# Reordering the first and the fourth turn of a two-layer graph attention kernel

## The chip, the cores and the metric

The kernel runs on one core of a Trainium2 chip. The metric is the device time of one execution in microseconds (us), as the median over runs. The core has five engines that run on their own and wait for each other through semaphores: TensorE (PE in the profile, with its weight loads as PEld), VectorE (DVE), ScalarE (ACT), GpSimd (POOL) and SyncE (SP), which here issues every DMA.

## The reference, cut to what matters

Two layers run one after the other on x of shape (128, 128, 512) in float32, with a Boolean mask `adj` of shape (128, 128, 128). Each layer is attention over the 128 nodes of each of the 128 graphs, a residual sum and a normalisation.

```python
# layer 0: 4 heads of 64
q, k, v = split_heads(x @ Wq), split_heads(x @ Wk), split_heads(x @ Wv)
sim  = where(adj, (q @ k.T) * 64 ** -0.5, -finfo.max)
x    = layernorm(x + softmax(sim) @ v @ Wo + bo)
# layer 1: 8 heads of 64, with a layernorm of its own ahead
h    = layernorm(x) * gamma + beta
q, k, v = split(h @ w_qkv.T, 3)
s    = where(adj | eye, (q @ k.T) * 64 ** -0.5, -1e9)
x    = layernorm(x + softmax(s) @ v @ w_out.T + b_out)
```

## The kernel before, in words

Two graphs make a group, so there are 64 groups. The kernel is a software pipeline of turns, written out by hand: the recording order of the calls is the order of the instructions on each engine, and nothing is reordered later. `opening` (L878) holds the first three turns, `step(s)` (L961) each turn from the fourth (s = 3) to s = 63, and three closing functions the rest. In turn s a step makes layer 0's q, k and v of group s, the scores and softmax of group s-1, the attention output of group s-2, and layer 1's q, k, v of group s-3. The fourth turn is special: layer 1 starts in it, so layer 1's weights are still being prepared.

Each product of a matrix by a weight is cut into seven half-sized products, numbered 1 to 7, of sums of halves (a Winograd scheme). For layer 0 `product_0(g, i, ts=...)` (L505) issues the matmuls of product i; `ts` says which of q (0), k (1) and v (2). In the first three groups q, k and v have matmuls of their own; afterwards one matmul covers all three. The products are added up in three banks of PSUM: bank a takes 1, 6, 7 and 4 in turn, bank c takes 2, bank f takes 5 and 3. Between two products the bank is read ("tapped") by `taken_0` (L539): ScalarE copies it for products 1, 5, 6 (L553) and 4 (L555), and VectorE adds a kept copy for products 2, 3 and 7 (L558). A matmul that writes a bank waits for all reads of that bank that were recorded ahead of it. `hold=True` puts a read off until `flush(HELD)`, so that it is recorded later.

The sums of halves come from two helpers. `sums` (L364) has GpSimd make four of them from a group's transposed x (L376: the third and fourth instruction make the operands of products 3 and 7, the second that of product 6, the first that of 5). `weight_sums_0((t, i), ...)` (L249) has VectorE make the four sums of a weight t in order (L255 in `combine`, i = 0 to 3): i = 0 replaces an operand of product 5, i = 1 makes that of product 6, i = 2 of 7, and i = 3 of 4. `weight_sums` (L235, recorded as L247) does the same for layer 1, block 0 on GpSimd and block 1 on VectorE. ScalarE scales Wq by 1/8 in the opening (L890).

Other pieces that the change touches: `transposed(g)` (L107, recorded as L114) turns x of group g in VectorE's 32 x 32 blocks. `load_quarters(g)` (L95) issues the four DMAs that bring that x, into a buffer that the transposes of the group before must have left. `more_loads` (L218) issues the loads that come after. `turn_weights(n)` (L199, recorded as L194) turns n of 12 blocks of layer 1's weights on VectorE. `masked`, `maxima`, `exps`, `normalised` and `blocks` are the steps of the softmax of one part: VectorE copies the scores under the mask (L653) and takes the negated maxima (L659), ScalarE makes eight exponentials (L668), VectorE the reciprocal (L676), GpSimd the multiplication (L677), and VectorE the block transpose (L695), which goes through device memory and comes back for the attention product. `out_product(0, g, i, ...)` (L560, matmuls at L581) is the same seven-product scheme for the output weight; after each one VectorE adds the bank to the residual rows (L585), here called an output addition. `turn` (L287, transposes L292) and `arrive` (L296) send layer 1's normalised rows through device memory, and `finish` (L325) receives them on ScalarE. `stats` (L775) is the row statistics on VectorE, with roots on GpSimd (L789 to L804).

VectorE, ScalarE, GpSimd and SP work strictly in recorded order. In `step(3)` before the change, VectorE takes the maxima and the transposes of `turn(0)` ahead of the first output additions:

```python
maxima(s, 0, 1)
if s == 3:
    turn(s - 3)
    arrive(s - 3)
...
out_product(0, s - 2, 1, 2, 5)
```

Of the kernel before, what the change touches and what calls it, by code (L numbers as in the profile page):

```python
# [17 lines left out]
P = 128  # L18
# [9 lines left out]
def kernel(ctx: ExitStack, tc: tile.TileContext, x, adj, wq, wk, wv, wo, bo,  # L28
                            gamma, beta, w_qkv, w_out, b_out, out):
    nc = tc.nc  # L30
# [26 lines left out]
    def flush(what=later):  # L57
        while what:
            what.pop(0)()
# [19 lines left out]
    def load_rows(g):  # L79
        if 0 <= g < NG and g not in R:  # L80
            R[g] = five.tile([P, G, E], F32, tag="r", name=f"r_{g}")
            nc.sync.dma_start(R[g], x[g * G:(g + 1) * G].rearrange("b n e -> n b e"))
# [63 lines left out]
    wsqk = const.tile([P, 3, KH, I1], F32, name="wsqk")  # L146
# [52 lines left out]
    def turn_weights(n):  # L199
        for _ in range(n):  # L200
            blocks_in.pop(0)()
# [3 lines left out]
    load_mask(0)  # L205
    load_blocks(KQ.rearrange("p a w b c j -> p (a w b c j)"), 0, 4)
    wo0 = const.tile([P, INNER[0] // P, E], F32, name="wo0")
    nc.sync.dma_start(wo0, wo.rearrange("(c p) f -> p c f", p=P))
    bias0, bias1 = (const.tile([P, E], F32, name=f"bias{i}") for i in range(2))
    gb_raw = one.tile([2 * KC, P], F32, tag="sm2", name="gb_raw")  # L210
    gb = const.tile([P, 2 * KC], F32, name="gb")
# [5 lines left out]

    def more_loads():  # L218

        load_rows(0)  # L220
        nc.sync.dma_start(bias0, bo[None, :].to_broadcast([P, E]))
        load_mask(1)
        load_blocks(wsqk.rearrange("p i c f -> p (i c f)"), 4, 10)
        for i, of_feature in enumerate((gamma, beta)):
            nc.sync.dma_start(gb_raw[i * KC:(i + 1) * KC].rearrange("c (a i) -> c a i", i=32),
                              of_feature.rearrange("(a c i) -> c a i", a=4, i=32))
        load_rows(1)
        load_blocks(wsv.rearrange("p i c f -> p (i c f)"), 10, 12)
        load_transposed(wo1, w_out, "w_out", 0, 1, 2, 3)
        nc.sync.dma_start(bias1, b_out[None, :].to_broadcast([P, E]))  # L230
# [18 lines left out]
    def weight_sums_0(*which):  # L249

        for t, i in which:
            b11, b12, b21, b22 = (w0[:, c:c + KH, t, h] for c in (0, KH) for h in range(2))
            t2, t3, t4 = (ws0[:, j, :, t] for j in range(3))
            o, a, b = ((b12, b12, b11), (t2, b22, b12), (t3, t2, b11), (t4, b21, t2))[i]
            nc.vector.tensor_tensor(o, a, b, op=ALU.subtract)  # L255
# [108 lines left out]
    def sums(l, g):  # L364
        if not 0 <= g < NG:
            return
        xs = XS[l, g] = one.tile([P, 4, KH, N], F32, tag="xs1" if g == 1 else f"xs{l}", name=f"xs{l}_{g}")
        halves_sums(xs, XT[l, g].rearrange("p (h c) (b n) -> p b h c n", h=2, b=2))
# [134 lines left out]
    HELD = []  # L503
# [374 lines left out]
    def opening():  # L878

        sums(0, 0)  # L880

        k, qv = (1,), (0, 2)
        product_0(0, 1, ts=k)
        product_0(0, 2, ts=k, hold=True)
        weight_sums_0((1, 0), (1, 1))
        product_0(0, 5, ts=k)
        product_0(0, 3, ts=k, hold=True)
        product_0(0, 6, ts=k)
        for h in range(2):
            nc.scalar.activation(w0[:, :, 0, h, :], w0[:, :, 0, h, :], AF.Copy, scale=SCALE)  # L890
        weight_sums_0((1, 2), (1, 3))
        product_0(0, 7, ts=k)
        product_0(0, 1, 2, ts=(0,), take=())
        product_0(0, 4, ts=k)
        flush(HELD)
        weight_sums_0((0, 0), (2, 0))
        product_0(0, 1, 2, ts=(2,), take=qv)
        weight_sums_0((0, 1), (2, 1), (0, 2), (2, 2), (0, 3), (2, 3))
        product_0(0, 5, 6, ts=qv)
        transposed(1)  # L900
        product_0(0, 3, ts=qv)
        load_quarters(2)
        more_loads()
        sums(0, 1)
        cleared(1, 0)
        product_0(0, 7, ts=qv)
        product_0(1, 5)
        turn_weights(4)
        product_0(0, 4, ts=qv)

        product_0(1, 2, hold=True)
        product_0(1, 1)
        made = scores(1)
        cleared(2, 0)
        masked(made, 1, 0)
        maxima(1, 0)
        product_0(1, 6)
        product_0(1, 3, hold=True)
        transposed(2)
        sums(0, 2)  # L920
        load_ahead(3)
        flush(HELD)
        exps(1, 0, 0, 1)
        product_0(1, 7)
        product_0(2, 5)
        product_0(1, 4)
        normalised(1, 0)
        weight_sums_out(0)
        product_0(2, 2, hold=True)
        made = scores(2)  # L930
        load(2)
        blocks_direct(1, 0)
        masked(made, 2, 0)
        addend(0, 0)
        product_0(2, 1)
        maxima(2, 0)
        attend(2)
        out_sums(0, 0)
        product_0(2, 6)
        flush(HELD)  # L940
        cleared(3, 0)
        turn_weights(2)
        exps(2, 0, 0)
        out_product(0, 0, 1, 2, 5)
        product_0(2, 3)
        exps(2, 0, 1)
        out_product(0, 0, 6)
        normalised(2, 0)
        addend(0, 1)
        product_0(2, 7)  # L950
        out_product(0, 0, 3, 7)
        stats(0, 0, 0)
        product_0(2, 4)
        out_product(0, 0, 4)
        blocks_direct(2, 0)
        turn_gamma_beta()
        stats(0, 0, 1)
        transposed(3)
        turn_weights(2)

    def step(s):  # L961

        made = scores(s)
        if s > 3:
            sums(0, s)
            arrive(s - 3)
        if s > 3:
            flush()
        load_ahead(s + 1)
        load_rows(s - 1)  # L970
        masked(made, s, 0, 1, 2)
        attend(s)
        if s == 3:
            flush()
        maxima(s, 0, 1)
        if s == 3:
            turn(s - 3)
            arrive(s - 3)
        out_sums(0, s - 2)
        if s == 3:  # L980
            flush(latest)
            sums(0, s)
        if s > 3:
            exps(s, 0, 0)
        product_0(s, 1)
        exps(s, 0, *((0, 1) if s == 3 else (1,)))
        out_product(0, s - 2, 1, 2, 5)
        maxima(s, 2)
        product_0(s, 2)
        normalised(s, 0)  # L990
        out_product(0, s - 2, 6, 3)
        exps(s, 1, 0)
        stats(0, s - 2, 0)
        product_0(s, 6)
        exps(s, 1, 1)
        out_product(0, s - 2, 7)
        if s == 3:
            turn_weights(2)
        blocks(s, 0)
        if s == 3:  # L1000
            weight_sums(w1qk, wsqk, 0)
        product_0(s, 5)
        out_product(0, s - 2, 4)
        normalised(s, 1)
        finish(s - 3, 0)
        stats(0, s - 2, 1)
        exps(s, 2, 0)
        product_0(s, 7)
        finish(s - 3, 1)
        exps(s, 2, 1)  # L1010
        probs_arrive(s, 0)
        blocks(s, 1)
        product_0(s, 3)
        if s == 3:
            addend(0, s - 1)
            weight_sums(w1qk, wsqk, 1)
            turn_weights(2)
        product_0(s, 4)
        transposed(s + 1)
        turn_qk0(s)  # L1020
        if s == 3:
            prepare(len(setup))
        normalised(s, 2)
        qk(s - 3, 1)
        flush()
        qk(s - 3, 2)
        blocks(s, 2)
        arrive_qk0(s)
        probs_arrive(s, 1)
        qk(s - 3, 6)  # L1030
        if s == 3:
            weight_sums(w1v, wsv, 0)
        qk(s - 3, 5)
        flush(latest)
        addend(1, s - 5)
        out_sums(1, s - 5)
        qk(s - 3, 7)
        if s == 3:
            weight_sums(w1v, wsv, 1)
        qk(s - 3, 3, 4)  # L1040
        kq_arrive(s - 3)
        if s < NG - 1:
            probs_arrive(s, 2)
        out_product(1, s - 5, 1, 2)
        v(s - 3, 1, 2)
        turn(s - 2)
        if s == NG - 1:
            probs_arrive(s, 2)
        cleared(s + 1, 0, 1, 2)
        v(s - 3, 6)  # L1050
        out_product(1, s - 5, 6, 5)
        v(s - 3, 5)
        if s == 4:
            weight_sums_out(1, 0)
        out_product(1, s - 5, 7, 3, 4)
        q0_in_order(s)
        q_in_order(s - 3)
        if s > 3:
            addend(0, s - 1)
        v(s - 3, 7)  # L1060
        if s == 4:
            weight_sums_out(1, 1, 2)
        stats(1, s - 5, 0)
        v(s - 3, 3)
        if s == 4:
            weight_sums_out(1, 3)
        stats(1, s - 5, 1)
        v(s - 3, 4)
        for g in (0, 1) if s == 3 else (s - 2,):
            with_self(g)  # L1070
        if s == NG - 1:
            arrive(s - 2)
            addend(1, s - 4)
# [197 lines left out]
```

## Time and profile before

| what | value |
|---|---|
| runs | 2729.40, 2729.04, 2727.89 us |
| median of the runs | 2729.04 us |
| the profiled execution: its own time | 2727.97 us |
| its span in the trace | 2726.2 us |
| busy: PE, DVE, POOL, ACT | 2713.4, 2032.4, 1752.4, 1507.1 us |
| instructions | 47796 |

The profile is of one execution, 1.07 us below the median of the runs and within their spread of 1.5 us; 1.8 us of its time lies outside the span. A busy time is the sum of an engine's instructions. TensorE is busy for all but 12.8 us of the span, so a stretch of the trace says most by how long TensorE sat idle in it and by which engine let it go on. In the rows of the timeline the first number is the start, the second the length, both in us; "x4" means that four records are merged in one row, and a bracket at the end gives the idle time ahead and the engine that ended it.

### The profile page before, as it was taken

The numbers are of one execution on the slowest core, as the hardware profiler recorded it, in microseconds if no ns is written. First come the engines' busy times: TensorE is split into PE (matmuls) and PEld (weight loads), VectorE is DVE, ScalarE is ACT, GpSimd is POOL, SyncE is SP. The second block draws the span as 40 slices with busy tenths as digits, with TensorE's granted clock in tenths as the row PEclk, the third lists the DMA queues.
The fourth block names the chain that finished last, engine by engine and source line by source line (L and its number), as shares of the span: only waits on it lengthen the run. The fifth ranks groups of instructions, "written<-read, shape, count | busy, mean of one in ns | idle before, by whom it ended". The sixth has DMA issues, their size and how long they took to land.

```text
span 2726.2 us, 47796 instructions
## 1 busy us (share of the span) xinstructions
PE 2713.4 (100%) x14901; PEld 1927.3 (71%) x14901; DVE 2032.4 (75%) x3678; ACT 1507.1 (55%) x4804; POOL 1752.4 (64%) x2315
## 2 busy tenths in 40 slices
PE   8999999999999999999999999999999999999999
PEld 7866767667667676676776766767767667677698
DVE  7777777777777777777777777777777777777765
ACT  3456455465564554655646556556465565564654
POOL 5566666666666666667666666676666666666674
PEclk9999999999999999999999999999999999999999
DMA  8577777878777778787777777877777777777751
GB/s 188 149 215 212 220 214 203 225 209 217 214 209 217 215 209 224 207 219 210 209 219 216 209 221 208 220 211 209 217 214 211 223 206 218 214 208 219 208 151 67
DMA packets 588900, 562.64 MB, mean 206 GB/s; under 512 B 59368, under 2 KB 539112, under 8 KB 588648
## 3 DMA queue, kind: packets, MB, share of 16 engines
q1 hardware_dynamic: 588648, 559.59, 73.6%
q8 instruction: 120, 1.97, 0.3%
q14 instruction: 132, 1.08, 0.1%
HBM read 300.95 MB, written 258.47 MB: 205 GB/s over the span
## 4 chain that ended last, share of the span: by engine, by line
PE 98%; DVE 1%; issue 0%; POOL 0%; ACT 0%; DMA 0%; POOLq 0%; DVEq 0%; ACTq 0%; SPq 0%
PE qka L413 16%; PE a L531 12%; PE oa L581 12%; PE va L413 8%; PE qkf L413 8%; PE av L748 6%; PE of L581 6%; PE f L531 6%; PE vf L413 4%; PE qkc L413 4%; PE oc L581 3%; PE c L531 3%; PE sc L615 2%; PE sc L621 2%; PE vc L413 2%; PE sc_a L621 2%
## 5 line engine op out<-in xcount | busy, mean ns | idle before, releaser
L668 ACT ACTIVATE sm<-sm,nmax 128x128 f32<-128x128 f32 x1536 | 595.2, 393 | 4.1 <-DVE nmax L659 2.5
L677 POOL TENSOR_TENSOR sm<-sm,rec 128x1024 f32<-128x1024 f32 x192 | 364.3, 1897 | 334.7 <-DVE rec L676 331.3
L770 POOL TENSOR_TENSOR r<-r,bias 128x1024 f32<-128x1024 f32 x128 | 301.6, 2357 | 128.2 <-ACT r L769 128.2
L585 DVE TENSOR_TENSOR r<-oa,r 128x256 f32<-128x256 f32 x508 | 212.2, 418 | 159.7 <-PE oa L581 125.7
L668 ACT ACTIVATION_READ_ACCUMULATOR sm<-sm,nmax 128x1 f32 x1536 | 295.2, 192 | 0.0
L423 ACT COPY ev<-va 128x256 f32<-128x256 f32 x128 | 47.6, 372 | 432.8 <-PE va L413 432.7
L695 DVE STREAM_TRANSPOSE turnedp<-sm 128x1024 f32<-128x1024 f32 x188 | 233.4, 1241 | 62.3 <-POOL sm L677 59.2
L789 POOL TENSOR_SCALAR ve<-mv 128x2 f32<-128x2 f32 x191 | 41.8, 219 | 367.1 <-DVE mv L782 356.5
L815 ACT ACTIVATE r<-r,shift,root 128x512 f32<-128x512 f32 x254 | 193.0, 808 | 123.9 <-POOL shift L804 123.9
L659 DVE TENSOR_REDUCE nmax<-sm 128x8 f32<-128x1024 f32 x192 | 226.5, 1206 | 0.3
L413 PE MATMUL qkf<-w,xs 128*128 128x512 f32 x472 | 221.8, 592 | 0.0
L413 PE MATMUL qka<-wsqk,xs 128*128 128x512 f32 x472 | 221.8, 592 | 0.0
L581 PE MATMUL oa<-wso,so 128*128 128x256 f32 x760 | 205.8, 379 | 1.8 <-POOL xs L376 1.7
L581 PE MATMUL of<-wo,so 128*128 128x256 f32 x760 | 205.7, 379 | 0.3 <-DVE r L585 0.2
L376 POOL TENSOR_TENSOR xs<-xT 128x256 f32<-128x256 f32 x256 | 187.4, 732 | 22.7 <-DVE xT L114 21.2
L653 DVE COPY_PREDICATED sm<-m,sc 128x512 f32<-128x512 uint8 x256 | 172.4, 728 | 12.9 <-issue 4.2
L531 PE MATMUL f<-w,xs 128*128 128x384 f32 (+1 forms) x512 | 181.0, 476 | 0.0
L531 PE MATMUL a<-ws,xs 128*128 128x384 f32 (+1 forms) x512 | 181.0, 476 | 0.0
L581 PEld LDWEIGHTS oa<-wso,so 128*128 128x128 f32 x760 | 143.6, 190 | 48.0 <-POOL xs L376 2.3
L781 DVE BATCH_NORM_STATS2 st<-r 128x6 f32<-128x512 f32 x254 | 174.9, 688 | 2.2
L639 POOL MEMSET sm<- 128x1024 f32 x192 | 175.1, 952 | 1.4 <-DVE turnedp L695 1.4
L413 PEld LDWEIGHTS qka<-wsqk,xs 128*128 128x128 f32 x472 | 89.7, 190 | 112.9 <-issue 112.9
(176 smaller groups left out, 6312.5 us busy)
## 6 DMA issues: line engine op xcount, KB each, us to landing
scrp<-turnedp SPq DMA_DIRECT2D x188, 512.0 KB, 3.3
pT<-scrp SPq DMA_DIRECT2D x752, 128.0 KB, 3.5
kq<-scrkq SPq DMA_DIRECT2D x236, 192.0 KB, 3.9
x<-in_x_dram SPq DMA_DIRECT2D x256, 128.0 KB, 3.8
r<-in_x_dram SPq DMA_DIRECT2D x64, 512.0 KB, 4.2
out_dram<-r SPq DMA_DIRECT2D x63, 512.0 KB, 3.6
scr<-turned SPq DMA_DIRECT2D x62, 512.0 KB, 4.1
kq<-scr SPq DMA_DIRECT2D x248, 128.0 KB, 2.8
```

The source lines that it names most:

```text
L376: nc.gpsimd.tensor_tensor(o, a0, a1, op=op)
L413: nc.tensor.matmul(o, lhsT, rhs, start=first and m == 0, stop=m == len(todo) - 1, skip_group_check=True)
L531: nc.tensor.matmul(o, lhsT, rhs, start=first and n == 0, stop=n == len(todo) - 1, skip_group_check=True)
L581: nc.tensor.matmul(acc, left[:, c], right[:, c], start=first and c == 0, stop=c == hk - 1, skip_group_check=True)
L585: nc.vector.tensor_add(part, acc, part)
L639: nc.gpsimd.memset(sm, NEG1 if part else NEG0)
L659: nc.vector.tensor_reduce(NMAX[s, part], SM[s, part], AX.X, ALU.max, negate=True)
L668: nc.scalar.activation(sm[:, i, k, :], sm[:, i, k, :], AF.Exp, bias=nmax[:, i, k:k + 1], accum_out=total[:, i, k:k + 1])
L677: nc.gpsimd.tensor_tensor(SM[s, part], SM[s, part], rec[:, :, :, None].to_broadcast([P, 2, K1, N]), op=ALU.mult)
L695: nc.vector.transpose(t.rearrange("p q (h r) -> p q h r", r=32), SM.pop((s, part)).rearrange("p i k (q r) -> p q (i k) r", r=32))
L770: nc.gpsimd.tensor_tensor(R[g], R[g], (bias0, bias1)[l][:, None, :].to_broadcast([P, G, E]), op=ALU.add)
L815: nc.scalar.activation(R[g][:, b], R[g][:, b], AF.Identity, bias=shift[:, b:b + 1], scale=root[:, b:b + 1])
```

## The change

In the opening, for group 0, ScalarE's scaling of Wq moves ahead of its copy of product 6, product 6 moves ahead of product 3, and the q products 1 and 2 are issued ahead of k's product 7. The v products 1 and 2 are issued apart, around k's product 4, and the addition after product 2 is held. Group 1's transposes come ahead of four of the weight subtractions, and the held additions behind those. Group 2's transposes come a good deal earlier, and group 1's product 3 is not held any more. The load of Wo moves behind the loads of group 2's x. Two block transposes of layer 1's weights leave the end of the opening for the fourth turn.

In the fourth turn the maxima come behind the first three output additions, the exponentials behind product 2, `turn` and `arrive` behind the next two output additions, the normalisation behind two weight transposes, and GpSimd's first four weight sums behind the second statistics and two more weight transposes. From the fifth turn on nothing is changed.

```diff
     wo0 = const.tile([P, INNER[0] // P, E], F32, name="wo0")
-    nc.sync.dma_start(wo0, wo.rearrange("(c p) f -> p c f", p=P))
...
     def more_loads():
 
+        nc.sync.dma_start(wo0, wo.rearrange("(c p) f -> p c f", p=P))
         load_rows(0)
...
         product_0(0, 5, ts=k)
-        product_0(0, 3, ts=k, hold=True)
-        product_0(0, 6, ts=k)
         for h in range(2):
             nc.scalar.activation(w0[:, :, 0, h, :], w0[:, :, 0, h, :], AF.Copy, scale=SCALE)
+        product_0(0, 6, ts=k)
+        product_0(0, 3, ts=k, hold=True)
+        product_0(0, 1, 2, ts=(0,), take=())
         weight_sums_0((1, 2), (1, 3))
         product_0(0, 7, ts=k)
-        product_0(0, 1, 2, ts=(0,), take=())
+        weight_sums_0((0, 0), (2, 0))
+        product_0(0, 1, ts=(2,), take=qv)
+        product_0(0, 2, ts=(2,), take=qv, hold=True)
         product_0(0, 4, ts=k)
-        flush(HELD)
-        weight_sums_0((0, 0), (2, 0))
-        product_0(0, 1, 2, ts=(2,), take=qv)
-        weight_sums_0((0, 1), (2, 1), (0, 2), (2, 2), (0, 3), (2, 3))
+        weight_sums_0((0, 1), (2, 1))
         product_0(0, 5, 6, ts=qv)
         transposed(1)
-        product_0(0, 3, ts=qv)
         load_quarters(2)
         more_loads()
+        weight_sums_0((0, 2), (2, 2), (0, 3), (2, 3))
+        flush(HELD)
+        product_0(0, 3, ts=qv)
         sums(0, 1)
...
         product_0(0, 4, ts=qv)
+        transposed(2)
...
         product_0(1, 6)
-        product_0(1, 3, hold=True)
-        transposed(2)
+        flush(HELD)
+        product_0(1, 3)
         sums(0, 2)
         load_ahead(3)
-        flush(HELD)
...
         transposed(3)
-        turn_weights(2)
 
     def step(s):
...
         if s == 3:
             flush()
-        maxima(s, 0, 1)
-        if s == 3:
-            turn(s - 3)
-            arrive(s - 3)
+        if s > 3:
+            maxima(s, 0, 1)
         out_sums(0, s - 2)
...
         product_0(s, 1)
-        exps(s, 0, *((0, 1) if s == 3 else (1,)))
+        if s > 3:
+            exps(s, 0, 1)
         out_product(0, s - 2, 1, 2, 5)
-        maxima(s, 2)
+        maxima(s, 2 if s > 3 else 0)
         product_0(s, 2)
-        normalised(s, 0)
+        if s > 3:
+            normalised(s, 0)
+        else:
+            exps(s, 0, 0, 1)
         out_product(0, s - 2, 6, 3)
+        if s == 3:
+            turn(s - 3)
+            arrive(s - 3)
         exps(s, 1, 0)
...
         if s == 3:
             turn_weights(2)
+            normalised(s, 0)
         blocks(s, 0)
-        if s == 3:
-            weight_sums(w1qk, wsqk, 0)
         product_0(s, 5)
         out_product(0, s - 2, 4)
         normalised(s, 1)
         finish(s - 3, 0)
         stats(0, s - 2, 1)
+        if s == 3:
+            turn_weights(2)
+            weight_sums(w1qk, wsqk, 0)
         exps(s, 2, 0)
```

## The prediction

> **What bounds the kernel now.** I read the page's chain of waits first, then the busy times by stage, then the timeline of the stages in which TensorE (PE) idles.
>
> ```profile
> span 2726.2 us, 47796 instructions
> ...
> PE 98%; DVE 1%; issue 0%; POOL 0%; ACT 0%; DMA 0%; POOLq 0%; DVEq 0%; ACTq 0%; SPq 0%
> ```
>
> ```profile
> 8.00:20.30 12.30, 9.79 (x78) 8.76 (x76) 8.56 (x21) 3.22 (x9) 2.68 (x4) 1.00 1.18 226
> 20.30:36.80 16.50, 15.76 (x149) 15.12 (x149) 11.49 (x17) 5.95 (x22) 9.96 (x11) 1.00 1.03 209
> 36.80:50.00 13.20, 13.20 (x110) 12.18 (x108) 11.32 (x21) 6.22 (x22) 8.34 (x8) 1.00 1.03 228
> 50.00:69.30 19.30, 16.95 (x92) 11.51 (x92) 18.41 (x35) 9.80 (x29) 16.14 (x25) 1.00 0.39 118
> ```
>
> After each stretch and its length come the busy times of PE, PEld, DVE, ACT and POOL. PE idles 2.51, 0.74, 0.00 and 2.35 us here: 5.60 us, the most that the change can win. From 130 to 2600 us PE is busy 2470.00 of 2470.00 us, so every us by which PE is earlier or later at 69.3 us reaches the end unchanged. In the last stretch, DVE is busy 18.41 of 19.30 us: where PE idles there, DVE is the bound.
>
> ```profile
> 18.13 1.30 DVE L114 STREAM_TRANSPOSE xT<-x 128x512 f32<-128x512 f32 x2
> ...
> 19.50 0.72 POOL L376 TENSOR_TENSOR xs<-xT 128x256 f32<-128x256 f32 x1 [9.47 <-DVE xT L114]
> ...
> 20.28 1.16 PE L531 MATMUL f<-xs,w 128*128 128x128 f32 x8 [0.69 <-POOL xs L376]
> ...
> 31.51 1.13 PE L531 MATMUL f<-xs,w 128*128 128x128 f32 x8 [0.74 <-DVE qkv L558]
> ...
> 32.90 0.91 POOL L376 TENSOR_TENSOR xs<-xT 128x256 f32<-128x256 f32 x1
> 33.25 0.83 DVE L266 TENSOR_TENSOR wso<-wo 128x256 f32<-128x256 f32 x1
> ...
> 33.77 2.08 POOL L677 TENSOR_TENSOR sm<-sm,rec 128x1024 f32<-128x1024 f32 x1
> ...
> 34.12 2.00 DVE L266 TENSOR_TENSOR wso<-wso,wo 128x256 f32<-128x256 f32 x1
> ```
>
> Two PE waits of the opening stand here, and a rule of prices: a DVE subtraction from SBUF that takes 0.42 us alone ended 0.27 us after the POOL operation beside it (33.81 and 34.08; 35.85 and 36.12). Additions with a PSUM operand, and transposes, show no such delay.
>
> ```profile
> 55.26 1.22 DVE L659 TENSOR_REDUCE nmax<-sm 128x8 f32<-128x1024 f32 x1
> ...
> 56.39 1.29 DVE L292 STREAM_TRANSPOSE turned<-r 128x512 f32<-128x512 f32 x2
> ...
> 57.31 0.73 POOL L376 TENSOR_TENSOR xs<-xs,xT 128x256 f32<-128x256 f32 x1
> ...
> 57.61 0.38 DVE L585 TENSOR_TENSOR r<-oa,r 128x256 f32<-128x256 f32 x1
> ...
> 58.14 0.67 PE L581 MATMUL oa<-wso,so 128*128 128x256 f32 x2 [1.75 <-POOL xs L376]
> ...
> 60.01 1.90 POOL L677 TENSOR_TENSOR sm<-sm,rec 128x1024 f32<-128x1024 f32 x1 [0.48 <-DVE rec L676]
> ...
> 63.14 1.21 DVE L695 STREAM_TRANSPOSE turnedp<-sm 128x1024 f32<-128x1024 f32 x1
> ...
> 65.52 0.54 DVE L558 TENSOR_TENSOR qkv<-a,e 128x384 f32<-128x384 f32 x1
> ...
> 66.11 1.56 PE L531 MATMUL a<-ws,xT 128*128 128x384 f32 x4 [0.41 <-DVE qkv L558]
> ```
>
> The 1.75 us are put down to POOL, whose second sum ended at 58.04. Product 6 of the output does not read it; it writes the bank that DVE's first output addition reads until 57.99. DVE was late through the maxima and `turn`.
>
> **The opening, part by part.** All times are on before's clock. PE's pairs of matmuls follow each other at 0.45 us, 0.52 after a wait. Product 5 of k issues at 8.75 as now. Product 6 needs its weight sum (DVE, until 9.45): 9.58, then product 3 at 10.03, and the 0.45 us ahead of it goes. ScalarE scales Wq from about 9.85 (1.15 us; its load is in by 9.84, when a DMA that waits for it issues), and then copies product 6: 11.25. That is the new wait of q's product 1, with k's 7 queued behind: 11.40 against 12.58 before. Product 2 of q 11.92, k's 7 at 12.37, and DVE's addition until 13.38. Now v's product 1 waits for it: 13.48 (before 14.51), product 2 14.00, k's product 4 behind a copy of 0.37: 14.62, products 5 and 6 from 15.14 (before 15.51) until PE is free at 16.93 (17.54). So far 0.4 to 0.6 us are won, as four k waits fall into two.
>
> Then it is given back. DVE transposes group 1 at 15.0 to 16.4 (the x DMAs issued up to 9.84 land in 4.4 to 5.0 us). Behind them stand four subtractions, and behind those the held additions, for which product 3 now waits. But the transposes release POOL's four sums at 16.47, which before started at 19.50 when no subtraction was left. By the rows at 33 us one subtraction escapes (16.84), and each other ends 0.27 us behind a sum: about 17.6, 18.4 and 19.2. If they didn't meet, all four would take 1.5 us (17.46 and the row before it, 0.75 a pair): 17.9. The two additions end 0.45 us later, so product 3 issues at 19.7 to 19.8 (or 18.45) against 17.65, and group 1's product 5 four pairs later: 21.67 (or 20.3) against 20.28. Cost: +1.4 us, or 0 without the meeting. I take +1.4, as the pairing is that of the rows.
>
> The wait of 0.74 at 31.51 goes: group 2's transposes now run at about 24.8 instead of 29.16, its sums are done by 29.3, and product 3's addition follows at once, at 31.5. PE gets there at 21.67 + (30.61 - 20.28) = 32.00, so 0.90 of idle and restart are won: net +0.5. The output weight's subtractions (L266) meet POOL's long multiplication and addition one place earlier in their row, and end at about 39.2 against 38.63; the copy behind them gates the attention product. PE's wait there grows from about 0.1 to 0.35: +0.2. The moved load of Wo costs nothing: it issues near 18.5 instead of 13.71 and is read at 32.67, and this load landed in 7.5 us.
>
> **The fourth turn.** Two weight transposes leave its front, so DVE copies masks at 52.75 instead of 53.90. The output additions then come at 54.30, 54.79 and 55.17, as PE delivers them; the 1.75 us are gone. Maxima 55.5, product 2's addition 56.6, two output additions until 57.9. PE issues output products 6 and 3 at 56.2 and 56.7, and then waits for POOL's second sum, which is where it was: layer 0's product 6 at 58.15 against 59.51. So far 1.36 us are won.
>
> But DVE has the same work to do ahead of product 7's addition, plus two weight transposes that were done before: `turn` 57.95, statistics 59.17, output addition 60.2, transposes 60.5, reciprocal 61.72 (the exponentials end at 59.96). Only now can POOL normalise: 62.0 to 63.9. Before, DVE filled this time with statistics, an addition and weight transposes, and its block transpose at 63.14 found the result there since 61.91. Now the block transpose is next in the queue, and **DVE stands for 2 us**. Behind it: block transpose 63.97, output addition 65.1, statistics 65.5, weight transposes 66.35, and then product 7's addition, 67.57 to 68.11. PE has been ready for product 4 since 64.25 and issues it at 68.2, against 66.11: **+2.1 us**. All of the 1.36 is lost in that, since this wait ends last. Bounds: if the DVE steps ran without a gap from 52.75, 66.2 (+0.1); if POOL's multiplication took 2.08, +2.3.
>
> Behind that, POOL's weight sums (5.21 us) start behind the roots at 68.05 and now meet DVE's own four. They end at 73.3 to 73.7, and the second sum that the first layer-1 product 6 needs at about 75.1. PE is there 6.71 us after product 4, at 74.9: +0.2, bounds 0 and +0.8. `finish` is covered: `turn` ends 1.6 us later than before, and the first layer-1 product comes 2.1 us later.
>
> **Sum**: +0.5 + 0.2 + 2.1 + 0.2 = +3.0 on 2727.97: **2731.0 us**. The median of the runs is 1.07 above the profiled execution; against it the change is +0.07%, against its own execution +0.11%. Both are within 0.2% (5.5 us), about what a measurement of this kernel can tell from no change.
>
> **The rivals.** (1) The opening's subtractions escape the sums, because POOL starts later or x lands earlier: 1.4 us less, 2729.6. For it: DVE ran three such operations at 0.75 a pair when POOL was idle. (2) The gap of 3.7 to 4 us ahead of product 4 brings down the clock. In the tail the mean clock is 0.92 from 2720 to 2724 and 0.50 after, so it halved at about 2723.4, 2.9 us after the last matmul ended. If it takes 2.9 us of work to come back, half of that is lost: +1.4, 2732.4. Against it: the drop need not come at the same delay. [...] (3) Slower by over 0.2%: DVE's and POOL's layer-1 weight sums do not overlap at all, so that each POOL operation also waits for one of DVE's (0.69 each, L247). POOL then ends 4 x 0.69 = 2.8 us later, the sum for product 6 comes at 77.9, and PE waits 3 us: +5.8, 2733.8. It decides as soon as the sum is later than 74.9. Against it: in the opening POOL's 0.73 grew only to 0.78 and 0.90 beside subtractions. [...] (4) The change does what it says and DVE does not stand: product 4 at 66.2 or earlier, and without the opening's meeting 2727. A gain of 0.2% would need nearly all of the 5.60 us.
>
> **Chances.** Forecast 0.50, (1) 0.16, (2) 0.14, (3) 0.11, (4) 0.09, of which 0.01 is a gain over 0.2%. Slower by over 0.2% is (3) and a little of (2) with (3): 0.12; faster 0.01; within 0.87. The range leaves out (3)'s upper half and the lower half of (4): 2727.2 to 2734.5.
>
> **What would show it.** Right: in the changed trace PE's longest idle time in the fourth turn ends at layer 0's product 4 with DVE's L558 as releaser, after about 4 us; DVE idles 2 us ahead of L695 for POOL's L677; L255 subtractions of 0.8 us stand at 17 to 19 us beside L376; PE waits 2 to 3 us ahead of group 0's q and v product 3; none at group 2's product 5. Wrong: a block transpose that finds its data, subtractions of 0.42, or a clock below 1.00 between 60 and 75 us. It fails altogether if a stretch after 130 us shows PE idle.

## The result and the profile after

The changed kernel takes 2733.4 us in the median of 22 runs (2731.70 to 2734.69), the kernel before 2728.07 us (2727.68 to 2729.46, 22 runs). The ratio is 1.0017, with a 95% interval of 1.001 to 1.0024: 5.3 us slower by the medians, inside the 0.2% that were called no change, but with an interval that leaves 1 out.

The runs don't scatter evenly. Before has 15 runs at 2727.7 to 2728.4 and 7 at 2729.0 to 2729.5; the changed kernel has 9 at 2731.7 to 2732.2, 9 at 2733.4 to 2733.6 and 4 at 2734.2 to 2734.7. Its lowest group stands 3.9 us above before's lowest, and the rest of the 5.3 us lies in how many executions fall into the higher groups. The profiled execution is one of the lowest group: 2731.89 us, of which the span is 2730.1. What follows compares it with the profiled execution of before (2727.97 us, span 2726.2): 3.9 us in both.

The busy times by stage in the changed kernel; the columns are as in the prediction, and behind the busy times come PE's granted clock (1.00 in all of them), the share of the DMA engines and GB/s.

```profile
8.00:20.30 12.30, 8.54 (x65) 7.50 (x65) 9.16 (x18) 3.22 (x9) 5.81 (x8) 1.00 1.20 210
20.30:36.80 16.50, 16.50 (x160) 16.12 (x159) 11.55 (x18) 5.84 (x22) 6.90 (x8) 1.00 1.15 238
36.80:50.00 13.20, 13.20 (x109) 12.04 (x106) 11.63 (x21) 5.82 (x22) 8.01 (x8) 1.00 0.91 210
50.00:72.00 22.00, 17.52 (x98) 12.18 (x97) 18.91 (x34) 10.32 (x30) 14.30 (x25) 1.00 0.37 116
72.00:92.70 20.70, 19.35 (x152) 18.07 (x152) 16.06 (x28) 6.16 (x12) 15.60 (x18) 1.00 0.23 84
...
130.00:2600.00 2470.00, 2470.00 (x13030) 1711.99 (x13027) 1857.35 (x3349) 1384.98 (x4418) 1603.80 (x2116) 1.00 0.77 214
```

PE idles 3.76 us in the first stretch (2.51 before), none in the second (0.74), 4.48 in the fourth and 1.35 in the fifth. From 130 us on it is busy throughout, as before: nothing is given back later.

The longest waits of PE in the changed kernel: who waited for whom, the total in us, how often, the longest.

```profile
PE a L531 <- DVE qkv L558: 4.1, 2, 3.6
PE f L531 <- DVE qkv L558: 2.6, 1, 2.6
PE qka L413 <- POOL xs L376: 1.4, 1, 1.4
PE ready L139 <- POOL mhalf L133: 1.3, 1, 1.3
PE a L531 <- POOL xs L376: 0.8, 1, 0.8
PE a L531 <- ACT e L553: 0.5, 1, 0.5
```

Three waits matter: 3.6 at layer 0's product 4 of the fourth turn, 2.6 at group 0's product 3, and 1.4 at layer 1's first product 6. (The 0.8, at layer 0's product 6, is what is left of before's wait of 1.75 just ahead of it; the 1.3 is the same in both.) Here is the second of the three in the timeline.

```profile
14.91 1.30 DVE L114 STREAM_TRANSPOSE xT<-x 128x512 f32<-128x512 f32 x2 [0.31 <-DMA x<-in_x_dram]
...
16.14 1.25 DVE L255 TENSOR_TENSOR ws<-ws,w 128x256 f32<-128x256 f32 x2
...
16.30 0.82 POOL L376 TENSOR_TENSOR xs<-xT 128x256 f32<-128x256 f32 x1 [6.25 <-DVE xT L114]
...
17.32 1.80 DVE L255 TENSOR_TENSOR ws<-w,ws 128x256 f32<-128x256 f32 x2
...
19.25 0.27 DVE L558 TENSOR_TENSOR qkv<-f,e 128x128 f32<-128x128 f32 x1
...
19.57 0.71 PE L531 MATMUL f<-xs,w 128*128 128x128 f32 x4 [2.59 <-DVE qkv L558]
...
21.46 1.08 PE L531 MATMUL f<-xs,w 128*128 128x128 f32 x8
...
31.70 1.06 PE L531 MATMUL f<-xs,w 128*128 128x128 f32 x8
```

A pair of subtractions takes 1.25 and 1.80 us beside the sums, and ends 0.27 and 0.29 us after a sum (16.30 + 0.82, 18.05 + 0.78). Before, GpSimd was idle beside them and a pair took 0.75:

```profile
17.46 0.75 DVE L255 TENSOR_TENSOR ws<-w,ws 128x256 f32<-128x256 f32 x2
```

Group 1's product 5 is at 21.46, 1.18 later than before; group 2's, without its wait, at 31.70, only 0.19 later. The fourth turn of the changed kernel:

```profile
62.09 0.16 DVE L676 RECIPROCAL rec<-total 128x8 f32<-128x8 f32 x1
62.33 1.90 POOL L677 TENSOR_TENSOR sm<-sm,rec 128x1024 f32<-128x1024 f32 x1 [2.39 <-DVE rec L676]
...
64.26 1.25 DVE L695 STREAM_TRANSPOSE turnedp<-sm 128x1024 f32<-128x1024 f32 x1 [2.01 <-POOL sm L677]
...
67.87 0.52 DVE L558 TENSOR_TENSOR qkv<-a,e 128x384 f32<-128x384 f32 x1
...
68.44 1.56 PE L531 MATMUL a<-ws,xT 128*128 128x384 f32 x4 [3.65 <-DVE qkv L558]
```

VectorE stands for 2.01 us in front of the block transpose, and everything behind it in its queue is late by that. Then the weight sums of the two engines, and PE's next wait:

```profile
69.72 1.61 POOL L247 TENSOR_TENSOR wsqk<-w 128x512 f32<-128x512 f32 x1
...
70.22 1.65 DVE L247 TENSOR_TENSOR wsqk<-w 128x512 f32<-128x512 f32 x1
...
71.40 1.59 POOL L247 TENSOR_TENSOR wsqk<-wsqk,w 128x512 f32<-128x512 f32 x1
...
71.91 1.64 DVE L247 TENSOR_TENSOR wsqk<-wsqk,w 128x512 f32<-128x512 f32 x1
...
75.89 0.73 POOL L376 TENSOR_TENSOR xs<-xs,xT 128x256 f32<-128x256 f32 x1
...
76.67 1.05 PE L413 MATMUL qka<-xs,wsqk 128*128 128x128 f32 x7 [1.35 <-POOL xs L376]
```

Before, the two rows of sums stood apart, and one such sum took GpSimd 1.27 us and VectorE 0.69:

```profile
63.22 1.27 POOL L247 TENSOR_TENSOR wsqk<-w 128x512 f32<-128x512 f32 x1
...
67.66 0.69 DVE L247 TENSOR_TENSOR wsqk<-w 128x512 f32<-128x512 f32 x1
...
72.82 1.95 PE L413 MATMUL qka<-xs,wsqk 128*128 128x128 f32 x16
```

Layer 1's first product 6 was at 72.82 and is at 76.67. That is 3.85 us, so practically the whole difference of 3.9 is there by then.

### The profile page after: what moved, and what is told of

Read it like the earlier page. It is cut to its first block, busy times and chain, and to the rows that moved or that the text cites. A ratio compares the mean times of both kernels' runs of the same rounds, so it can differ in the third digit from the quotient of the medians.

```text
span 2730.1 us, 47795 instructions
## 1 busy us (share of the span) xinstructions
PE 2713.1 (99%) x14901; PEld 1927.0 (71%) x14901; DVE 2035.6 (75%) x3678; ACT 1507.5 (55%) x4804; POOL 1753.0 (64%) x2315
## 4 chain that ended last, share of the span: by engine, by line
PE 98%; POOL 1%; DVE 0%; DMA 0%; issue 0%; SPq 0%; POOLq 0%; DVEq 0%
PE qka L413 16%; PE a L531 12%; PE oa L581 12%; PE va L413 8%; PE qkf L413 8%; PE av L748 6%; PE of L581 6%; PE f L531 6%; PE vf L413 4%; PE qkc L413 4%; PE oc L581 3%; PE c L531 3%; PE sc L615 3%; PE sc L621 2%; PE vc L413 2%; PE sc_a L621 2%
## 5 line engine op out<-in xcount | busy, mean ns | idle before, releaser
L815 ACT ACTIVATE r<-r,shift,root 128x512 f32<-128x512 f32 x254 | 193.0, 808 | 122.9 <-POOL shift L804 122.9
```

The source lines that it names most:

```text
L815: nc.scalar.activation(R[g][:, b], R[g][:, b], AF.Identity, bias=shift[:, b:b + 1], scale=root[:, b:b + 1])
```

## The experiments

The theory: three places make the loss, each by the order of the work and not by added work. In the opening the held additions stand behind subtractions that GpSimd's sums hold up; in the fourth turn VectorE stands in front of the block transpose; and then the weight sums of VectorE and GpSimd hold each other up. On top of these, PE's clock drops in some executions, in the gaps that were made. Rivals: one of the two turns carries the whole loss; VectorE simply has too much work in the fourth turn; the runs' groups have nothing to do with PE. Each median is set beside that of the kernel before on the same chip.

### Each turn alone

The opening alone is the changed kernel's opening with `turn_weights(2)` at its end, and before's `step`; the fourth turn alone is before's opening without that call, and the changed `step`.

> Only the opening is changed; the two weight transposes stay at its end, and the fourth turn is that of before. Theory: the opening wins 0.6 us by its earlier product waits and 0.9 at group 2's product 5, and gives back 1.2 to 1.4 at group 0's product 3, so that PE is 0.2 to 0.4 us later at 50 us: 2728.3 to 2728.6 where before is 2728.1. Rival (the opening carries the whole loss of the change, the fourth turn none): 2733.4.

> Only the fourth turn is changed, with the two weight transposes that it takes over; the opening is that of before. Theory: product 4 of layer 0 is 1.9 to 2.1 us later and layer 1's first product 6 another 1.4 to 1.5: +3.4 to +3.6, 2731.6 in undisturbed executions and 1.6 to 2.7 more where the clock drops in the gap of 3.6 us ahead of product 4. Rival (the opening carries the loss): 2728.1.

Measured: the opening alone 2730.04 us (2728.68 to 2731.64, 11 runs), before 2728.35 (27 runs), ratio 1.0006, interval 0.9997 to 1.0015. The fourth turn alone 2731.59 us (2731.26 to 2732.67, 11 runs), ratio 1.0013, interval 1.0004 to 1.0021. So both rivals fall: neither turn carries the whole. The fourth turn hit its number: 7 of its runs lie at 2731.3 to 2731.7. Its upper group, 2732.4 to 2732.7, is only 1.0 higher, where 1.6 to 2.7 were expected. The opening hit its number only in its best run, 2728.68; its median is 1.4 to 1.7 us over the expected span. In its trace PE gets to group 2's product 5 at 31.82, so 0.31 later than before, as the theory has it. The rest shows further on, behind the wait of the old fourth turn:

```profile
58.65 0.67 PE L581 MATMUL oa<-wso,so 128*128 128x256 f32 x2 [1.73 <-POOL xs L376]
59.51 0.83 PE L581 MATMUL of<-wo,so 128*128 128x256 f32 x2 [0.19 <-DVE r L585]
...
68.16 1.56 PE L531 MATMUL a<-ws,xT 128*128 128x384 f32 x4 [0.26 <-DVE qkv L558]
```

Product 4 is at 68.16 where 66.6 would follow. The same kernel by stretches (the third number from the right is the granted clock):

```profile
58.00:60.00 2.00, 1.16 (x4) 0.79 (x5) 1.72 (x5) 2.00 (x11) 1.92 (x3) 0.97 0.47 195
60.00:62.00 2.00, 2.00 (x4) 1.04 (x4) 1.61 (x4) 0.21 (x2) 1.54 (x2) 0.50 0.18 70
62.00:64.00 2.00, 2.00 (x6) 1.33 (x5) 0.55 (x3) 0.48 (x1) 1.92 (x3) 0.67 0.83 252
```

The clock is halved from about 59.9 to 63.3 us, behind a gap of 1.7. The 1.5 us by which product 4 is late is about what a halved clock over these 3.4 us costs (an estimate: half of it, 1.7). That is the prediction's clock rival, at a place that it had not named, and the runs on the clock below test it.

### The block transpose later

```diff
         if s == 3:
             turn_weights(2)
             normalised(s, 0)
-        blocks(s, 0)
+        else:
+            blocks(s, 0)
...
         product_0(s, 7)
+        if s == 3:
+            blocks(s, 0)
         finish(s - 3, 1)
```

> The changed kernel, with the block transpose of the fourth turn recorded behind product 7, so that VectorE no longer stands in front of product 7's addition until GpSimd has normalised. Theory (VectorE's standing makes the gap ahead of product 4): the addition is 3 us earlier, PE's wait there falls from 3.65 to 0.5 to 1 us, but GpSimd's roots and weight sums are moved up by less, so that 1.5 to 2 us wait remain at layer 1's first product 6: 2.4 us less than the changed kernel, 2729.4 to 2730. Rival (the gap is made by the amount of work, two more weight transposes of 1.3 us ahead of the addition): the wait stays over 2.4 us and the time within 1 us of 2731.9.

Measured: 2729.49 us (2729.25 to 2731.33, 11 runs), before 2728.35, ratio 1.0005, interval 0.9996 to 1.0014. PE's waits in its trace:

```profile
65.38 1.56 PE L531 MATMUL a<-ws,xT 128*128 128x384 f32 x4 [0.51 <-DVE qkv L558]
74.22 2.05 PE L413 MATMUL qka<-xs,wsqk 128*128 128x128 f32 x16 [1.96 <-POOL xs L376]
```

The wait at product 4 falls from 3.65 to 0.51 with the same instructions on VectorE ahead of it, save the block transpose: of the 3.14 us, 2.01 were the standing and most of the rest the transpose's own 1.25. So VectorE was not simply full: the two weight transposes are still ahead of the addition. Product 4 is 3.06 us earlier, but layer 1's product 6 only 2.45, as its wait grows from 1.35 to 1.96. That second wait is what the next run is about.

### The weight sums apart

```diff
-                    eng=nc.gpsimd if w is w1qk and c == 0 else nc.vector)
+                    eng=nc.vector)
...
             turn_weights(2)
-            weight_sums(w1qk, wsqk, 0)
...
-            weight_sums(w1qk, wsqk, 1)
+            weight_sums(w1qk, wsqk, 0, 1)
```

> The changed kernel, with all eight of layer 1's weight sums for q and k on VectorE, in one row where VectorE had its four, so that GpSimd has none and can't meet them. Theory (the wait of 1.35 us at layer 1's first product 6 comes from the two engines' sums holding each other up): GpSimd's second sum is ready by 71 us, the wait goes, VectorE's eight take 5 to 6 us against 6.4 for the four now, and the time is 1.3 us less than the changed kernel. Rival (the wait comes from the late arrival of layer 1's rows): the wait of 1.35 stays and the time with it. Third: VectorE's longer row makes a later product wait, and the time is the same or up to 1 us more though the first wait is gone.

Measured: 2738.25 us (2737.87 to 2740.03, 5 runs), before 2728.35, ratio 1.0039, interval 1.0025 to 1.0053. This is a miss in the time: the expected 1.3 us less than the changed kernel's lowest group became 6.4 more. Its first half came as the theory had it: GpSimd's second sum ended at 70.5, and PE had no wait at layer 1's product 6. But VectorE's row took 9.5 us, not 5 to 6, as it met GpSimd's sums of x and then the addition of the bias, which held one subtraction for 2.84 us:

```profile
72.74 2.80 POOL L770 TENSOR_TENSOR r<-r,bias 128x1024 f32<-128x1024 f32 x1
...
73.25 2.84 DVE L247 TENSOR_TENSOR w<-w 128x512 f32<-128x512 f32 x1
...
85.31 0.68 DVE L500 SCALAR_TENSOR_TENSOR qo<-qka,eqk 128x512 f32<-128x512 f32 x1
...
86.04 3.58 PE L413 MATMUL qka<-xT,wsqk 128*128 128x128 f32 x16 [1.99 <-DVE qo L500]
```

Everything behind it on VectorE was late, and layer 1's product 4 waited 1.99 us for an addition, the third case of the expectation in a larger size. And the clock fell twice: the four matmuls of layer 0's product 4 took 2.10 us instead of 1.56 (the clock is 0.81, 0.50 and 0.84 in the stretches from 68 to 74 us), and the product after the wait took 3.58 instead of 1.95 (the clock is 0.57 in both stretches from 86 to 90 us). These losses don't make up the whole 6.4 either: set beside the changed kernel's, the trace is 3.86 us late at 131 us, 4.9 at about 1307 and 6.3 at the end. What adds 2.4 us over the later turns stays open.

The run shows that the wait of 1.35 came from GpSimd's row of weight sums, and that this is no way to mend it. As GpSimd has no row left here, it can't tell by itself whether the row was late by the meeting or by its own length. The rows of the changed kernel do: without growth it would have ended at 68.37 + 5.21 = 73.58, and the second sum of x, 1.53 later by before's rows, at about 75.2, when PE was there (75.3). A kernel further below shows the two cases side by side.

### The clock

Matmuls of the identity, into a bank that nothing reads, fill the gaps and leave nothing out; the second kernel has both lines, the first only that of the fourth turn.

```diff
+    def fill(n, name):
+        warm = mm_tile(name)
+        for _ in range(n):
+            nc.tensor.matmul(warm[:, :P], ident, ident, start=True, stop=True, skip_group_check=True)
...
         flush(HELD)
+        fill(9, "warm_open")
         product_0(0, 3, ts=qv)
...
             weight_sums(w1qk, wsqk, 1)
             turn_weights(2)
+            fill(14, "warm_turn")
         product_0(s, 4)
```

> The changed kernel, with 14 matmuls of the identity into an unread bank recorded ahead of product 4 in the fourth turn, about 3.2 us of work that fills most of the gap of 3.65 us there. It adds work and leaves nothing out. Theory (the executions at 2733.4 and 2734.6 are those in which PE's clock drops in a gap): if this gap is the cause, runs gather at 2731.7 to 2732.2 and those at a mean clock of 0.998 are gone or few. Rival (the spread of 3 us has another cause, as a DMA or the launch): the three groups stay as they are. Third: the gap in the opening causes part, and the group at 2733.4 stays while the one at 2734.6 goes.

> As the run before, with 9 more such matmuls, about 2 us, ahead of group 0's q and v product 3 in the opening, where PE idles 2.6 us. Theory: all runs within 0.5 us of 2731.9, as no gap over 1.5 us is left before the tail. Rival (neither gap has to do with the spread): three groups up to 2734.6.

Measured: with the fourth turn's gap filled 2733.49 us (11 runs), with both filled 2731.89 (11 runs), before 2728.30. By single runs: with one gap filled, 3 runs at 2731.7 to 2731.9 and 8 at 2733.0 to 2733.7, none higher; with both, all 11 at 2731.65 to 2732.16. The third case of the first expectation is what came: the highest group goes with the fourth turn's gap, the middle one with the opening's. The first half of that is the weaker one: 4 runs of 22 became 0 of 11, which chance alone would give in about one case of nine. That no run of 11 is left in either upper group with both gaps filled, where 13 of 22 were, can hardly be chance: the spread comes from the two gaps, and traces show PE's clock drop at them. The profiled execution of the first kernel is one of the middle group (2733.49 us) and shows the drop:

```profile
18.00:20.00 2.00, 0.49 (x4) 0.49 (x5) 1.79 (x5) 0.00 (x0) 2.00 (x3) 1.00 1.22 210
20.00:22.00 2.00, 2.00 (x16) 2.00 (x15) 0.42 (x1) 0.00 (x0) 1.42 (x2) 0.73 1.18 197
22.00:24.00 2.00, 2.00 (x12) 2.00 (x11) 1.90 (x4) 0.00 (x0) 0.00 (x0) 0.50 1.04 348
24.00:26.00 2.00, 2.00 (x18) 2.00 (x18) 1.40 (x3) 0.85 (x2) 0.00 (x0) 0.92 1.09 338
```

From the means the clock is halved from about 20.9 to 24.3 us, 3.4 us long, and begins 1.4 us after PE has gone back to work at 19.5, behind a gap of 2.45 us in this run. By an estimate it costs half of 3.4 us, 1.7, and the groups are 1.6 apart.

The last run on this takes the kernel before and fills its wait of 1.75 us, with `fill(7, "warm_turn")` ahead of `out_product(0, s - 2, 6, 3)` in the fourth turn.

> The kernel before, with 7 matmuls of the identity into an unread bank, about 1.6 us, recorded ahead of the output products 6 and 3 of the fourth turn, where PE waits 1.75 us; nothing is left out. Theory (the kernel before also has executions in which the clock drops in a gap, and this is the gap): the runs at 2729.0 to 2729.7 go, and all lie at 2727.6 to 2728.5. Rival (they come from somewhere else, as the opening or the tail): both groups stay.

Measured: 2727.98 us, all 11 runs at 2727.72 to 2728.25, while the unchanged kernel on the same chip had 6 of 20 at 2729.2 to 2730.2. So before's upper group came from that gap; that the clock was the reason is argued from the other traces, as none of before's was taken in that group.

### The opening and the fourth turn mended

In the opening, on the changed kernel:

```diff
-        weight_sums_0((0, 2), (2, 2), (0, 3), (2, 3))
         flush(HELD)
+        weight_sums_0((0, 2), (2, 2))
         product_0(0, 3, ts=qv)
...
         product_0(1, 5)
+        weight_sums_0((0, 3), (2, 3))
         turn_weights(4)
```

> The changed kernel with the held additions ahead of the weight subtractions again, and the four subtractions split in two pairs, each ahead of the product that needs it. Theory (product 3 waits for additions that stand behind subtractions that GpSimd's sums hold up): product 3 issues at about 17.0 instead of 19.57, group 1's product 5 at 18.9 instead of 21.46, and everything after is 2.3 to 2.6 us earlier: 2729.4 in undisturbed executions. Rival (the additions are late because the transposes are, not because of the subtractions): product 3 stays over 18.5 and the gain is under 1 us.

Measured: 2730.69 us (2729.28 to 2731.20, 11 runs), before 2728.30, ratio 1.0007, interval 0.9998 to 1.0016. Product 3 issues at 16.99 and group 1's product 5 at 19.64, so 1.82 us earlier and not 2.3 to 2.6: product 7 still waits a little for subtractions beside GpSimd's sums (a pair takes 1.85). The best run lies at the expected 2729.4, the median above it, and the profiled execution (2731.19) shows why: the gap ahead of product 4 is still there, and this time the clock falls inside it, at about 65.4, and stays halved until 72.2, so for 6.8 us (means of 0.84, three times 0.50, and 0.95 in the stretches from 64 to 74 us).

```profile
61.51 1.45 PE L531 MATMUL f<-w,xs 128*128 128x384 f32 x4
66.61 2.93 PE L531 MATMUL a<-ws,xT 128*128 128x384 f32 x4 [3.65 <-DVE qkv L558]
69.34 3.30 PE L156 MATMUL w_outt<-ident,raw_v 128*128 128x128 f32 x16
72.48 1.95 PE L413 MATMUL qka<-xT,w 128*128 128x128 f32 x16
```

The two rows take 5.87 us from start to start where the changed kernel's took 3.14 (68.44 to 71.58). Of the 2.7 us lost, about half costs nothing, as layer 1's product 6, which would have waited 1.35, waits no more.

Then the fourth turn, on top of that kernel:

```diff
         if s == 3:
-            flush(latest)
             sums(0, s)
+            flush(latest)
...
-            turn_weights(2)
             normalised(s, 0)
-        blocks(s, 0)
+            turn_weights(4)
+            weight_sums(w1qk, wsqk, 0)
+        else:
+            blocks(s, 0)
...
-        stats(0, s - 2, 1)
-        if s == 3:
-            turn_weights(2)
-            weight_sums(w1qk, wsqk, 0)
+        if s > 3:
+            stats(0, s - 2, 1)
...
         finish(s - 3, 1)
+        if s == 3:
+            blocks(s, 0)
+            stats(0, s - 2, 1)
```

> The kernel of the run before, and in the fourth turn: normalisation ahead of the weight transposes, all four of these in one row, GpSimd's weight sums right behind its multiplication, block transpose and second statistics behind product 7, the sums of x ahead of the ratios. Theory: the waits at product 6 (0.84), product 4 (3.65) and layer 1's product 6 (1.35) go, and one of up to 0.8 us comes at layer 1's first product, which waits for the rows that go through device memory: 2724 us, 4 us less than before. Rival (VectorE is simply full in the fourth turn, so that a wait taken away comes back at the next product): no better than before, 2728.

Measured: 2726.06 us (2725.48 to 2727.19, 11 runs), before 2728.30, ratio 0.9992, interval 0.9984 to 1.0001. The three waits are gone; 2.2 of the 4 us came. Three of GpSimd's weight sums now run ahead of VectorE's and keep their length (1.27, 1.27 and 1.28 us). The fourth still meets them, and grows as in the changed kernel:

```profile
63.20 1.28 POOL L247 TENSOR_TENSOR wsqk<-wsqk,w 128x512 f32<-128x512 f32 x1
...
64.44 1.72 POOL L247 TENSOR_TENSOR wsqk<-w,wsqk 128x512 f32<-128x512 f32 x1
...
65.07 1.65 DVE L247 TENSOR_TENSOR wsqk<-w 128x512 f32<-128x512 f32 x1
```

So the meeting makes the growth. Of the 1.8 us that didn't come, 1.1 went into a wait that was not foreseen: the later statistics made GpSimd's roots late, ScalarE's normalisations (L815) wait for them, and ScalarE's copy of layer 1's product 6 stands behind these.

```profile
PE qka L413 <- ACT eqk L425: 1.1, 1, 1.1
```

The last kernel records the `flush()` of the normalisations behind layer 1's product 7 instead of behind product 1 (s = 3 alone).

> The kernel mended in both turns, with the layer 0 normalisations of the fourth turn on ScalarE recorded behind layer 1's product 7 instead of behind product 1. Theory (in the mended kernel PE waits 1.12 us for ScalarE's copy of layer 1's product 6, which stands behind normalisations that wait for late roots): the wait goes and the time is 1.0 to 1.1 us less, 2725.0. Rival (the copy is late for another reason, or the next product waits in its place): 2726.0.

Measured: 2724.84 us, all 11 runs at 2724.48 to 2725.20, before 2728.22 (20 runs), ratio 0.9986, interval 0.9977 to 0.9995. Its longest waits of PE are 1.3 us at the very start and 0.5; from 50.0 to 69.3 us PE is busy 19.08 of 19.30. It beats both kernels: 3.4 us under before, about 8.6 under the changed one.

## Why the prediction was right, and where it was off

**The chain to the forecast held.** The opening wins early, loses at group 0's product 3 and wins at group 2's product 5: it is 0.19 us late at 31.70 and 0.40 late at 50 us, where +0.7 was forecast (+0.5 and +0.2). Both ends were forecast 0.2 to 0.3 us too late: product 5 of group 1 at 21.46 for 21.67, of group 2 at 31.70 for 32.00. The meeting of subtractions and sums is there in the rows; taking the two apart gave 1.8 us. The signs that were named for being right are all in the trace.

**The fourth turn's standing** came as forecast: layer 0's product 6 at 58.50 (58.15 and the 0.40), VectorE idle 2.01 us (forecast 2), product 7's addition at 67.87 (67.57 plus the 0.40 by which PE came late is 67.97), product 4 at 68.44, PE's wait 3.65. That is 1.93 us on top of the opening's, forecast +2.1. The run with the block transpose later shows the cause.

**The mis-sized term is the layer-1 weight sums**: forecast +0.2 with bounds of 0 and +0.8, measured +1.52 (3.85 less 2.33), so outside its own bounds. The place and the mechanism were right. The price was taken from the opening, where GpSimd's operation of 0.73 grew to 0.78 and 0.90; here its 1.27 grew to 1.59 to 1.72, so that its row ended at 74.68 instead of 73.3 to 73.7, and the first sum of x behind it took 1.17 beside VectorE's last subtraction. VectorE's operations here are longer (0.69 alone against 0.42), and a POOL operation that met one grew by about half of it. The rival with full exclusion (+2.8 on the row) was too dear in turn: the row grew from 5.21 to 6.31. One VectorE and one GpSimd operation in turn, without overlap, would be 0.69 + 1.27 = 1.96 us a pair, by an estimate from their lengths in the kernel before. The sums start 1.56 to 1.69 us after each other in both rows, so about half of the way to full exclusion; which part of an operation overlaps with the other's is not shown.

**The sum** for an execution with an undisturbed clock was +3.0 on the profiled execution's own time, and +3.9 came. The median of the runs moved by 5.3, because the clock rival (0.14) is not a rival but an addition, by the filled gaps in 13 of 22 executions. The step that failed there is in its condition: one gap was named, that of product 4, with a drop 2.9 us behind the last matmul. The opening's gap of 2.6 us was worked out in the same text and not counted, and before's 1.75 us, too, go with an upper group of about a third of the executions. In two traces the clock was halved for 3.4 us (59.9 to 63.3 with the opening alone, 20.9 to 24.3 with the fourth turn's gap filled), behind gaps of 1.73 and 2.45 us. Half of 3.4 us, 1.7, is an estimate of the loss, and agrees with the 1.6 between the groups.

The range held the time with little to spare, 2733.4 under 2734.5, and that is partly luck: its upper end had been left for a part of rival (3), and what used it up was a loss 0.9 larger than forecast with the clock undisturbed, and about 1.5 more by the clock. The 0.87 for no change held just as narrowly, 5.3 us against a bound of 5.5. The runs tell the two kernels apart better than that: the interval of the ratio begins at 1.001. The +0.07% was reckoned against a median of three runs, two of which lay in before's upper group; of 22 runs the median is 2728.07, close to the profiled execution.

**Left open**: which of the middle group's executions had a drop in the opening and which a long one in the fourth turn. The opening's gap gave 1.6 us; the fourth turn's, where it stood alone, 1.0 by the groups of its runs, or nothing. Only profiled executions show which it was. Open, too, are the 2.4 us that the kernel with all sums on VectorE lost over its later turns.

## What to carry to other kernels

In a queue that works in strict order, the price of an instruction that must wait is paid by everything recorded behind it (here VectorE stood for 2.01 us, and PE's wait behind it grew from 0.41 to 3.65 us): ask what stands there and who needs that, before asking how long the wait is. When an edit brings two engines' rows side by side that were apart before, price them by a pair that was caught side by side with operations of the same length. Here a gap on TensorE of 1.7 to 3.7 us cost its own length and, in a share of the executions, 1.0 to 1.6 us more, so count all gaps, and look at single runs and not the median alone.

## What was not expected of the hardware

The clock dropped behind gaps shorter than the 3.4 us for which it then stayed halved: 1.73 us of waiting (then halved from 59.9 to 63.3 us) and 2.45 us, where the drop began 1.4 us after PE had resumed. With that wait of the fourth turn filled by about 1.6 us of matmuls of the identity, the kernel before lost its upper group (none of 11 runs, where 6 of 20 were in it).

One drop was free: in the fourth turn the slow matmuls used up time that the next product would have waited anyway, so the kernel with the fourth turn alone shows a halved clock from about 69.5 to 72.9 us (means of 0.87, 0.50 and 0.78 in the stretches from 68 to 74) in an execution of 2731.55 us, in its lowest group.

GpSimd and VectorE held each other up less than in full: 1.27 and 0.69 us apart, 1.6 to 1.8 us each side by side, where one after the other they would take 1.96 (1.27 + 0.69, an estimate). Transposes, additions with an operand in PSUM and masked copies on VectorE kept their lengths beside GpSimd's sums: a pair of transposes took 1.30 us beside one (at 61.92 in the kernel before) and 1.30 with GpSimd idle (at 18.13 there), an addition 0.42 (at 58.10 there) and 0.42 (at 60.53 in the changed kernel), a pair of masked copies 1.35 (at 27.75 in the changed kernel) and 1.35 (at 26.64 in the kernel before).
